# Window attention after a gated scan: exponentials head by head with a bias and a running sum, a residual folded into a product, small square roots on another engine, other planner settings

## The chip, the cores and the metric

The kernel runs on one core of one Trainium2 chip. The metric is the device time of one execution in microseconds (us). All data is 32-bit float. TensorE is PE in the profile's rows (PEld its weight loads), VectorE is DVE, ScalarE is ACT, GpSimd is POOL, and SyncE, which here only issues DMAs, is SP.

## The reference

Two layers in a row on x of 8 images x 192 channels x 64 x 64. The first projects to 384 channels, takes a 3x3 convolution by channel, makes gates from a 16-wide proxy, and runs a recurrence over 8 steps in four directions, each step reading the state of the row above, of its own and of the row below. Its outputs are summed over the directions, normed over the channels (layernorm, then GRN, a norm over the whole image), and projected back to 192. The second layer works on windows of 8x8 tokens with six heads of 32:

```python
def _layer_norm(x, g, b):
    mu = jnp.mean(x, -1, keepdims=True)
    var = jnp.mean(jnp.square(x - mu), -1, keepdims=True)
    return (x - mu) * jax.lax.rsqrt(var + EPS_LN) * g + b
...
shortcut = _layer_norm(xs, norm1_g, norm1_b)
...
attn = jnp.einsum('bhnd,bhmd->bhnm', _l2n(q), _l2n(k)) * temperature
kth = jax.lax.top_k(attn, IN_CC)[0][..., -1:]
attn = jnp.where(attn >= kth, attn, NEG)
...
attn = jax.nn.softmax(attn + rpb[None], axis=-1)
out = jnp.einsum('bhnm,bhmd->bhnd', attn, v)
...
out = out @ proj_w.T + proj_b
...
x2 = shortcut + out
hdn = _layer_norm(x2, norm2_g, norm2_b)
hdn = jax.nn.gelu(hdn @ fc1_w.T + fc1_b, approximate=False) @ fc2_w.T + fc2_b
x2 = x2 + hdn
```

`IN_CC` is 16, `NEG` is -100.

## The kernel before

**Stages.** For image 0 a prologue does the convolution with the input in SBUF: by VectorE for nine units of 16 rows x 128 channels (`convolved`, L477 and L479), by PE with diagonal weights for three (`convolved_by_products`, L489). From then on three generators write down steps for every image: `front` (projection and convolution of the next images, through a padded copy in DRAM), `scan` (the recurrence) and `window_row` (the second layer for one row of eight windows, 512 tokens; eight such rows an image, 64 in all). The windows of an image can begin only when its scan has ended, since GRN needs the whole image: while image b is scanned, the windows of image b-1 are worked on. After the last scan only windows are left.

**The planner.** `Plan` takes each step with its engine, an assumed cost, and what it reads and writes. `run` simulates the engines with these costs, and gives each engine the ready step of lowest rank; a step that is late by more than SLACK is passed over. `order` repeats this RUNS times, each time with ranks moved towards the latest start that the step's users allow, and keeps the order of the shortest plan. The instructions are then issued in that order on every engine. So the order is fixed when the kernel is built, and each engine works through its own queue in it. Buffers are given out by the same plan: PSUM has two banks for `nb` and six shared ones (`lp`, and `g` in the scan).

**A scan tile** (128 channels, one direction, one step; 96 an image): PE makes gates (`project`, L808) into PSUM; ACT takes their absolute values (L865, L887), VectorE multiplies gates by the state (L872, L874), POOL adds (L896, L913, L917), ACT takes a reciprocal through Ln and Exp (L909, L911), VectorE and POOL multiply (L924, L928, L933), VectorE writes the state (L941). For two tiles at a time PE makes the output gates, VectorE multiplies (L967, L972), and POOL adds to the sum (L979 to L989).

**A window row.** Lines that the change or the prediction touches:

- `zg` is read and scaled on ACT (L1171). PE projects tokens into PSUM `pz` (L1186). VectorE writes `s0 = pz * n1_g` (L1193), ACT squares `pz` with a running sum `ss` (L1205; reading the sum is an instruction of its own), two 128-token groups at a time.
- `rsqrt` is an inverse square root: Ln, Exp and Square on ACT (L613 to L615), then three small Newton instructions on POOL (L618 to L620). It is used for `ss` and `sd` (twice a row each, two columns), for `nn` (once a row, 48 columns) and for `gr` (once an image). Scaling by 1/192 and adding 1e-5 are POOL's (L1211, L1536).
- ACT scales `s0` by `ss` (L1219); PE transposes it into `sT` (L1151), of which there is one; `s0` has two buffers, since the residual still needs it.
- q and k are projected (L1236), normed and transposed; scores go from PSUM to `at` (L1365), 24 pairs of columns (three groups of two heads times eight windows), 64 wide.
- For each of three groups: VectorE finds the 16 largest (L1378 to L1382) and masks the rest (L1392, L1395). POOL adds the position bias (L1405), negates the maximum into `down` (L1413) and adds it (L1422). ACT takes one exponential of 512 columns (L1426). VectorE sums (L1429) and inverts (L1430); POOL multiplies (L1437).
- PE transposes and attends (L1452, L1472), and projects `oT` into `pp` (L1506). VectorE adds the residual, `x2 = pp + s0` (L1518), and takes mean and variance (L1529, L1530). ACT negates the mean (L1546), POOL multiplies it by `sd` (L1553), ACT norms (L1561).
- The MLP follows: transposes (L1574, L1576), two products with a Gelu between them (L1593, L1597, L1604, L1613), and the second with the residual added by identity products (L1627), then the output (L1641).

After each scan VectorE computes GRN's scales with eight small instructions (L1109 to L1115 and L1128 to L1135).

Of the kernel before, what the change touches and what calls it, by code (L numbers as in the profile page):

```python
# [82 lines left out]
class Plan:  # L83
# [9 lines left out]
    RUNS = 60  # L93
    SLACK = 40.0
# [56 lines left out]
    def order(self):  # L151
# [9 lines left out]
        for n in range(self.RUNS):  # L161
# [7 lines left out]
            for s in run:  # L169
                needs = [d.start for d in s.after] + [h.next.start for h in s.held if h.next]  # L170
                rank = min(needs, default=s.end) - (s.end - s.start)
                s.rank = (s.rank + rank) / 2 if n else rank
# [152 lines left out]
def tile_ss2d_then_window_attention(ctx: ExitStack, tc: tile.TileContext, a: dict, out: bass.AP):  # L325
# [62 lines left out]
    n1_g = load("n1_g", a["n1_g"].partition_broadcast(P))  # L388
# [25 lines left out]
    sT, oT = (blank(n, [P, 2, GT], 0.0) for n in ("sT", "oT"))  # L414
    for t in (sT, oT):
        nc.gpsimd.memset(t[HALF : HALF + 1, 1, :], 1.0)
# [11 lines left out]
    with early, tc.tile_pool(name="early_ps", bufs=2, space=PSUM) as early_ps:  # L428
# [53 lines left out]
        def convolved_by_products(ct, u):  # L482

            acc = epool.tile([P, 16, W], F32, name="acc_p", bufs=2)
# [11 lines left out]
        by_vector = [(ct, u) for ct, u in units if ct < CT - 1 or u == 0]  # L496
# [5 lines left out]
        for n, c in enumerate(by_vector):  # L502
            acc = convolved(*c)
            stored(*c, acc)
            if n in (4, 6, 7):
                convolved_by_products(CT - 1, (4, 6, 7).index(n) + 1)
# [53 lines left out]

        ps = prep_ps.tile([P, 512], F32, name="ps_pre")
# [7 lines left out]
        for ci in range(2):  # L569
            w = w_f1[:, ci, :]  # L570
            nc.vector.tensor_scalar(w, w, n2_g[:, ci : ci + 1], None, ALU.mult)
# [32 lines left out]
    def rsqrt(v, key, shape, name, gain=1.0):  # L604

# [5 lines left out]
        plan("ACT", tiny, lambda: nc.scalar.activation(r(), v(), AF.Ln), r=[key], w=[r])  # L613
        plan("ACT", tiny, lambda: nc.scalar.activation(r(), r(), AF.Exp, scale=-0.5, bias=log_c[gain]), w=[r])
        plan("ACT", tiny, lambda: nc.scalar.activation(sq(), r(), AF.Square), r=[r], w=[sq])  # L615

        def newton():
            nc.gpsimd.tensor_mul(v(), v(), sq())  # L618
            nc.gpsimd.tensor_scalar(v(), v(), -1.0, 3.0 * c * c, ALU.mult, ALU.add)
            nc.gpsimd.tensor_mul(v(), v(), r())  # L620

        plan("POOL", (750.0, 60.0), newton, r=[r, sq], w=[key])


    def front(b, xs, xsT):
# [48 lines left out]
        def convolve(ct, s):  # L674
# [30 lines left out]
            st = Held(fpool, [P, CH, 64], "st", bufs=2)  # L705
# [37 lines left out]
    def scan(b, xs, xsT, z, made):  # L743
# [371 lines left out]
        plan("DVE", tiny, lambda: nc.vector.tensor_mul(gn(), gn(), gr()), r=[gr], w=[gn])  # L1115
# [27 lines left out]
    def window_row(b, g, z, sc, bb):  # L1143
        def two_blocks(dst, key, src):

            for ci in range(2):
# [8 lines left out]
                plan("PE", turned(4), turn, r=[src], w=[pt])  # L1155
# [8 lines left out]

        zg = Held(lpool, [P, CT, CH, 64], "zg", bufs=1)
# [8 lines left out]
        s0 = Held(lpool, [P, NT, DM], "s0", bufs=2)  # L1174
        for t2 in range(2):
            pz = bank()
            ss = Held(small, [P, 2], "ss")
            for k in range(2):

                def tokens(t2=t2, k=k, pz=pz):  # L1180
# [10 lines left out]
                "DVE",  # L1191
                vec(2 * DM),
                lambda two=two, pz=pz: nc.vector.tensor_mul(  # L1193
                    s0()[:, two, :],
                    pz()[:, 0 : 2 * DM].rearrange("p (k m) -> p k m", k=2),
                    n1_g.unsqueeze(1).to_broadcast([P, 2, DM]),
# [5 lines left out]
            def squares(pz=pz, ss=ss):  # L1202
                for k in range(2):
                    part = pz()[:, k * DM : (k + 1) * DM]
                    nc.scalar.activation(part, part, AF.Square, accum_out=ss()[:, k : k + 1])  # L1205

            plan("ACT", (782.0, 100.0), squares, w=[pz, ss])
            plan(
                "POOL",
                tiny,  # L1210
                lambda ss=ss: nc.gpsimd.tensor_scalar(ss(), ss(), 1.0 / DM, 1e-5, ALU.mult, ALU.add),  # L1211
                w=[ss],
            )
            rsqrt(ss, ss, [P, 2], "ss")

            def scaled(t2=t2, ss=ss):
                for k in range(2):
                    part = s0()[:, 2 * t2 + k, :]
# [3 lines left out]
            yield  # L1222
        plan.lane = 7
        two_blocks(sT, "sT", s0)
# [5 lines left out]
        for tt in range(NT):  # L1230
# [9 lines left out]
            plan("PE", mm(2, DIN), projected, r=["sT"], w=[pq, (qk, "room")])  # L1240
# [27 lines left out]
        for p2 in range(2):  # L1268
# [14 lines left out]
            plan("PE", mm(4, DM), values, r=["sT"], w=[pv, (v, "room")])  # L1283
# [85 lines left out]
        for r in range(3):  # L1369
# [21 lines left out]
            def mask(rng=rng, less=less):  # L1391
# [19 lines left out]
                "POOL",  # L1411
                tiny,
                lambda rng=rng: nc.gpsimd.tensor_scalar(down()[:, rng], top()[:, rng, 0], -1.0, None, ALU.mult),  # L1413
# [5 lines left out]
            plan(  # L1419
                "POOL",  # L1420
                gp(512),
                lambda part=part, rng=rng, each=each: nc.gpsimd.tensor_add(part(), part(), each(down()[:, rng])),  # L1422
                r=[(down, r)],
                w=[(at, r)],
            )
            plan("ACT", act(512, 95.0), lambda part=part: nc.scalar.activation(part(), part(), AF.Exp), w=[(at, r)])  # L1426

            def denominators(part=part, rng=rng):
                nc.vector.tensor_reduce(rd()[:, rng], part(), AX.X, ALU.add)  # L1429
                nc.vector.reciprocal(rd()[:, rng], rd()[:, rng])  # L1430

            plan("DVE", (833.0, 83.0), denominators, r=[(at, r)], w=[(rd, r)])
# [63 lines left out]
        x2, xn = (Held(lpool, [P, NT, DM], n, bufs=1) for n in ("x2", "xn"))  # L1496
        for t2 in range(2):
            pp = bank()
            two = slice(2 * t2, 2 * t2 + 2)
            stats, mv, sd = Held(small, [P, 2, 6], "stats"), Held(small, [P, 2, 2], "mv"), Held(small, [P, 2], "sd")  # L1500

            def projected(t2=t2, pp=pp):
# [269 lines left out]
```

## Time and profile before

| | us |
|---|---|
| median of 3 runs | 7552.91 (7535.86 to 7554.57) |
| profiled execution, its own time | 7551.0 |
| its span, first to last instruction | 7549.2 |
| mean granted TensorE clock | 0.864 of full speed |

The page gives the busy time of each engine, the span in 40 slices, and groups of instructions by line. A group's row reads: line, engine, operation, output<-input (partitions x elements), count, then busy time and the mean of one, then how long the engine stood idle just before them and for whom. The slices show where the stages change:

```profile
PE   7888799898989899888999899989888888898887
PEld 3333344444444444444445444444444444444554
DVE  6787798988899889898898988889899988899543
ACT  3555377765676567675777757776666656666765
POOL 1898788998899989987988888889899989899422
PEclk8887699987988889898988889987888878888999
```

Each digit is a slice of 189 us in tenths; PEclk is the granted clock. The costliest groups that belong to the window rows' part under the change are small beside the scan's:

```profile
L896 POOL TENSOR_TENSOR ab<-ab 128x512 f32<-128x512 f32 x672 | 866.0, 1289 | 163.1 <-ACT ab L865 151.5
L1422 POOL TENSOR_TENSOR at<-at,down 128x512 f32<-128x512 f32 x192 | 201.7, 1051 | 3.5
L1429 DVE TENSOR_REDUCE rden<-at 128x8 f32<-128x512 f32 x192 | 129.4, 674 | 42.5 <-ACT at L1426 42.4
L1426 ACT ACTIVATE at<-at 128x512 f32<-128x512 f32 x192 | 121.1, 633 | 69.8 <-POOL at L1422 69.2
```

### The profile page before, as it was taken

The page shows a single profiled execution, that of the slowest core. Times are in us where ns is not written, and L with a number is a line of the kernel's source. Part 1 is how long each engine was busy: PE and PEld are TensorE (multiplying, and loading weights), DVE is VectorE, ACT ScalarE, POOL GpSimd, SP SyncE. Part 2 cuts the span into 40 slices and gives each one's busy share as a digit, 9 for nine tenths or more (in the row PEclk, how much of TensorE's full clock was granted, in tenths as well). Part 3 has the DMA queues.
Part 4 walks back from the last instruction along what each step waited for, and adds up shares of the span by engine and source line. Part 5 has one row for each costly group of instructions (what it writes and reads, how often), then busy time and mean ns, then how long its engine had stood idle before and what let it go on. Part 6 is the DMA issues. An engine that isn't in the chain of part 4 may idle for free. (4 is left out here: it accounts for less than half of the span.)

```text
span 7549.2 us, 141750 instructions
## 1 busy us (share of the span) xinstructions
PE 6680.5 (88%) x50180; PEld 3448.8 (46%) x50180; DVE 6360.6 (84%) x15477; ACT 4895.1 (65%) x9649; POOL 6227.8 (82%) x6333
## 2 busy tenths in 40 slices
PE   7888799898989899888999899989888888898887
PEld 3333344444444444444445444444444444444554
DVE  6787798988899889898898988889899988899543
ACT  3555377765676567675777757776666656666765
POOL 1898788998899989987988888889899989899422
PEclk8887699987988889898988889987888878888999
DMA  5666354313541246213641144411121121111110
GB/s 165 163 174 162 108 154 124 81 50 100 157 120 50 68 133 158 65 49 94 162 117 44 53 121 132 119 47 53 54 55 48 45 67 44 50 45 45 32 22 14
DMA packets 988330, 669.39 MB, mean 89 GB/s; under 512 B 651971, under 2 KB 814214, under 8 KB 987622
## 3 DMA queue, kind: packets, MB, share of 16 engines
q1 hardware_dynamic: 986486, 658.87, 32.5%
q8 instruction: 398, 6.52, 0.4%
q14 instruction: 310, 2.54, 0.1%
q10 hardware_dynamic: 1136, 1.47, 0.1%
HBM read 433.98 MB, written 226.18 MB: 87 GB/s over the span
## 5 line engine op out<-in xcount | busy, mean ns | idle before, releaser
L808 PE MATMUL g<-xe,w_g 32*128 32x512 f32 x3648 | 1165.2, 749 | 228.5 <-DVE dx L967 80.5
L808 PE MATMUL g<-xo,w_g 32*128 32x512 f32 x3648 | 1201.7, 730 | 186.3 <-DVE dx L967 95.6
L865 ACT ACTIVATE ab<-g 128x512 f32<-128x512 f32 x1344 | 784.9, 596 | 397.9 <-PE nb L808 169.6
L896 POOL TENSOR_TENSOR ab<-ab 128x512 f32<-128x512 f32 x672 | 866.0, 1289 | 163.1 <-ACT ab L865 151.5
L928 POOL TENSOR_TENSOR pw<-pw,rr 128x512 f32<-128x512 f32 x672 | 865.9, 1289 | 134.7 <-ACT rr L911 113.7
L913 POOL TENSOR_TENSOR pw<-pw,pq 128x512 f32<-128x512 f32 x672 | 881.6, 1312 | 77.7 <-DVE pq L872 52.0
L917 POOL TENSOR_TENSOR pw<-pw,pq 128x512 f32<-128x512 f32 x672 | 877.4, 1306 | 15.5
L909 ACT ACTIVATE rr<-nb,eps 128x512 f32<-128x512 f32 x672 | 461.9, 687 | 577.9 <-DVE nb L906 575.3
L981 POOL TENSOR_TENSOR dx<-dx,hu 128x512 f32<-128x512 f32 x576 | 743.0, 1298 | 111.0 <-DVE hu L972 94.2
L808 PEld LDWEIGHTS g<-xo,w_g 32*128 32x128 f32 x3648 | 412.8, 207 | 726.8 <-DVE dx L967 200.3
L808 PEld LDWEIGHTS g<-xe,w_g 32*128 32x128 f32 x3648 | 407.2, 212 | 702.9 <-DVE dx L967 179.4
L1627 PE MATMUL lp<-hd,w_f 128*64 128x256 f32 (+1 forms) x2304 | 604.7, 502 | 57.2 <-ACT hd L1613 15.0
L989 POOL TENSOR_TENSOR y<-y,dx 128x512 f32<-128x512 f32 x384 | 598.2, 1565 | 2.2
L695 PE MATMUL lp<-strip,w_cv 128*32 128x256 f32 x8064 | 566.8, 420 | 27.3 <-DMA strip<-pad 22.7
L924 DVE SCALAR_TENSOR_TENSOR nb<-nb,rr 128x512 f32<-128x512 f32 x672 | 464.0, 691 | 145.4 <-ACT rr L911 142.8
L933 DVE SCALAR_TENSOR_TENSOR nb<-nb,pw 128x512 f32<-128x512 f32 x672 | 463.6, 690 | 139.3 <-POOL pw L928 137.4
L906 DVE TENSOR_TENSOR nb<-nb,ab 128x512 f32<-128x512 f32 x672 | 464.1, 691 | 115.1 <-POOL ab L896 106.6
L972 DVE TENSOR_TENSOR hu<-g,hid 128x512 f32<-128x512 f32 x768 | 516.8, 678 | 0.9 <-PE g L808 0.6
L887 ACT ACTIVATE nb<-nb 128x512 f32<-128x512 f32 x672 | 399.5, 595 | 141.1 <-DVE pq L874 80.3
L808 PE MATMUL nb<-xe,w_g 32*128 32x512 f32 x672 | 479.1, 799 | 10.0 <-DVE hid L941 9.8
L808 PE MATMUL nb<-xo,w_g 32*128 32x512 f32 x672 | 464.1, 777 | 16.9 <-DVE hid L941 16.8
L941 DVE TENSOR_TENSOR hid<-lx,nb 128x512 f32<-128x512 f32 x672 | 454.2, 676 | 4.9
(223 smaller groups left out, 16413.8 us busy)
## 6 DMA issues: line engine op xcount, KB each, us to landing
strip<-pad SPq DMA_DIRECT2D x1008, 132.0 KB
xd<-xsT SPq DMA_DIRECT2D x384, 256.0 KB
x<-xs SPq DMA_DIRECT2D x64, 768.0 KB
xd<-xs SPq DMA_DIRECT2D x192, 256.0 KB
z<-y SPq DMA_DIRECT2D x64, 768.0 KB
zg<-z SPq DMA_DIRECT2D x64, 768.0 KB
pad<-xin SPq DMA_DIRECT2D x168, 264.0 KB
xsT<-sn SPq DMA_DIRECT2D x168, 256.0 KB
```

Of the source, the lines that this page charges most:

```text
L695: nc.tensor.matmul(pc()[q * RG : (q + 1) * RG, k * 256 : (k + 1) * 256].rearrange("p (h w) -> p h w", h=4), lhsT=w_cv[:, ct, q, dx, :], rh ...
L808: nc.tensor.matmul(dst, lhsT=w[rows, col : col + P], rhs=xp[rows, :], start=True, stop=True)
L865: lambda r=r: nc.scalar.activation(ab()[:, r, :], g[r](), AF.Abs),
L896: plan("POOL", gp(512), lambda: nc.gpsimd.tensor_add(ab()[:, 0, :], ab()[:, 0, :], ab()[:, 1, :]), w=[ab])
L906: plan("DVE", vec(512), lambda: nc.vector.tensor_add(nb(), nb(), ab()[:, 0, :]), r=[ab], w=[nb])
L913: plan("POOL", gp(512), lambda: nc.gpsimd.tensor_add(one(), one(), pq()[:, 0, :]), r=[(pq, 0)], w=[pw])
L917: lambda: nc.gpsimd.tensor_add(one(), one(), pq()[:, 1, :]),
L928: plan("POOL", gp(512), lambda: nc.gpsimd.tensor_mul(one(), one(), rr()), r=[rr], w=[pw])
L972: lambda: nc.vector.tensor_mul(like(hu(), d), like(pu(), d), state(d, ct)),
L981: plan("POOL", gp(512), lambda: nc.gpsimd.tensor_add(dx(), dx(), hu()), r=[hu], w=[dx])
L989: nc.gpsimd.tensor_add(y, y, dx().rearrange("p (c i) -> p i c", c=CH))
L1627: nc.tensor.matmul(dst[:, at : at + rhs.shape[-1]], lhsT=lhsT, rhs=rhs, **flags)
```

## The change

- **Exponential.** POOL's add of the negated maximum and VectorE's sum go. ACT takes 24 exponentials of 64 columns a row, eight to a step, each with its maximum as bias and its sum accumulated. The negation moves from POOL to VectorE, with a lower bound of -100 on the maximum.
- **Small square roots.** `rsqrt`'s Newton steps move from POOL to VectorE, two instructions in place of three, and give the negated result; the sign is taken back in weights (`n1_g`, `w_f1`, `gn`). Division and epsilon move into ACT's Ln and Square. `ss` and `sd` are treated once a row with four columns, not twice with two.
- **First norm.** `n1_g` is multiplied into weights beforehand; `s0` is a plain copy of `pz` on ACT.
- **Residual and second norm.** PE adds the residual: `sT` times a diagonal matrix `w_dg`, accumulated into `pp`; a 193rd column of both products gives the negated mean. ACT copies `x2` and the mean out of PSUM and takes the variance as a square with a running sum. `sT` gets a second buffer, `s0` and `st` lose theirs.
- **Prologue.** One more unit of the convolution on PE, one fewer on VectorE.
- **Planner.** 12 plans in place of 60, SLACK 80 in place of 40, ranks moved by 0.4 in place of 0.5.

```diff
-    RUNS = 60
-    SLACK = 40.0
+    RUNS = 12
+    SLACK = 80
...
-                s.rank = (s.rank + rank) / 2 if n else rank
+                s.rank = 0.6 * s.rank + 0.4 * rank if n else rank
...
-        by_vector = [(ct, u) for ct, u in units if ct < CT - 1 or u == 0]
+        by_vector = [(ct, u) for ct, u in units if ct < CT - 1]
...
         def newton():
-            nc.gpsimd.tensor_mul(v(), v(), sq())
-            nc.gpsimd.tensor_scalar(v(), v(), -1.0, 3.0 * c * c, ALU.mult, ALU.add)
-            nc.gpsimd.tensor_mul(v(), v(), r())
+            nc.vector.scalar_tensor_tensor(v(), v(), eps * mean, sq(), ALU.add, ALU.mult)
+            nc.vector.scalar_tensor_tensor(v(), v(), 3.0 * c * c, r(), ALU.subtract, ALU.mult)
-        plan("POOL", (750.0, 60.0), newton, r=[r, sq], w=[key])
+        plan("DVE", (160.0 + 4 * math.prod(shape[1:]) / 0.96, 85.0), newton, r=[r, sq], w=[key])
...
-                lambda rng=rng: nc.gpsimd.tensor_scalar(down()[:, rng], top()[:, rng, 0], -1.0, None, ALU.mult),
+                lambda rng=rng: nc.vector.tensor_scalar(down()[:, rng], top()[:, rng, 0], NEG, -1.0, ALU.max, ALU.mult),
...
-                lambda part=part, rng=rng, each=each: nc.gpsimd.tensor_add(part(), part(), each(down()[:, rng])),
-            plan("ACT", act(512, 95.0), lambda part=part: nc.scalar.activation(part(), part(), AF.Exp), w=[(at, r)])
-                nc.vector.tensor_reduce(rd()[:, rng], part(), AX.X, ALU.add)
+            for i0 in range(r * WS, (r + 1) * WS, 8):
+                def powers(i0=i0):
+                    for i in range(i0, i0 + 8):
+                        row = at()[:, i, :]
+                        nc.scalar.activation(
+                            row, row, AF.Exp, bias=down()[:, i : i + 1], accum_out=rd()[:, i : i + 1]
+                        )
+                plan("ACT", (290.0 * 8, 95.0), powers, r=[(down, r), (at, r)], w=[(at, r, i0), (rd, r, i0)])
...
+                    for j in range(2):
+                        cols = slice(at + j * HALF, at + j * HALF + more)
+                        nc.tensor.matmul(pp()[:, cols], lhsT=sT[:, j, tok], rhs=w_dg[:, j, :], start=False, stop=j == 1)
...
-                lambda two=two, pp=pp: nc.vector.tensor_add(
+                nc.scalar.copy(
+                    x2()[:, 2 * t2 : 2 * t2 + 2, :].rearrange("p k (j m) -> p k j m", j=2),
...
-                    nc.vector.bn_stats(stats()[:, k, :], x2()[:, 2 * t2 + k, :])
-                    nc.vector.bn_aggr(mv()[:, k, :], stats()[:, k, :])
+                    nc.scalar.activation(
+                        xn()[:, k, :], x2()[:, k, :], AF.Square, bias=less_m()[:, k : k + 1], accum_out=sd()[:, k : k + 1]
+                    )
```

## The prediction

> **What bounds the kernel now.** I read the page's busy line first, then the table of stages, then who VectorE waits for, then single rows.
>
> ```profile
> PE 6680.5 (88%) x50180; PEld 3448.8 (46%) x50180; DVE 6360.6 (84%) x15477; ACT 4895.1 (65%) x9649; POOL 6227.8 (82%) x6333
> ```
>
> Three engines are close together and ScalarE (ACT) has room. The stages, cut at the ends of the first and the last image's scan (found by the GRN reduction at L1109, at 938 and 7030 us):
>
> ```profile
> 60.00:938.00 878.00, 713.94 (x4537) 302.76 (x4536) 661.28 (x1017) 427.19 (x707) 657.26 (x519) 0.77 0.57 152
> 938.00:7030.00 6092.00, 5475.67 (x41528) 2849.64 (x41529) 5425.99 (x13275) 4116.09 (x8214) 5407.01 (x5457) 0.87 0.31 84
> 7030.00:7549.00 519.00, 437.72 (x3986) 277.12 (x3984) 228.41 (x1146) 327.40 (x698) 148.21 (x321) 0.93 0.10 21
> ```
>
> Columns: stretch, length, busy time of PE, PEld, DVE, ACT, POOL, granted clock, DMA. From 938 to 7030, where scan and windows overlap, PE is busy 90%, VectorE 89%, GpSimd (POOL) 89%, ACT 68%. In the last 519 us only windows run: PE 84%, ACT 63%, the two others under 45%. The change touches windows only, so the first 938 us hardly move. The same table for L1426 alone puts 164 of its 192 instructions (three to a window row) before 7030: 54.7 of the 64 rows lie in the middle stage, 9.3 in the tail. VectorE's longest waits in the middle stage:
>
> ```profile
> DVE nb L933 <- POOL pw L928: 105.4, 103, 4.8
> DVE nb L924 <- ACT rr L911: 103.2, 96, 5.4
> DVE nb L906 <- POOL ab L896: 69.7, 86, 4.4
> DVE pq L872 <- PE nb L808: 62.4, 55, 4.1
> ```
>
> Summed over all its waits there: POOL 193.2, ACT 206.5, PE 203.6 us. No engine alone is the bound; the scan's chain runs through all four.
>
> **The change, part by part, in busy time for a window row.** *POOL loses* the add of the negated maximum (L1422, 201.7 us over 64 rows), the negation (L1413, 59.0), every small Newton and scaling instruction of the three square roots (L618 to L620 on ss, sd and nn: 82.9, 76.9 and 52.1; L1211 26.0, L1536 28.1, L1553 25.4): 552.1, or 8.6 us a row, 470 in the middle stage. It falls there from 5407 to 4937, 81%.
>
> *VectorE loses* L1193 and L1518 (69.6 each), L1529 and L1530 (86.5, 46.5) and the sum over the powers, L1429 (129.4): 401.6, or 6.28 a row. *It gains* ten small instructions a row: two for each of three square roots, a product for less_m, three negations. Their price decides the case, and all ten are of a kind that this kernel hardly issues: every operand in SBUF, two of them in seven and one in the negations. The nearest are the scales after a scan:
>
> ```profile
> 950.36 1.18 DVE L1131 TENSOR_TENSOR sc<-sc,vecs 128x3 f32<-128x3 f32 x1
> 951.58 1.19 DVE L1132 TENSOR_SCALAR sc<-sc 128x3 f32<-128x3 f32 x1
> ```
> ```profile
> 950.26 1.27 POOL L896 TENSOR_TENSOR ab<-ab 128x512 f32<-128x512 f32 x1
> 951.48 1.27 POOL L981 TENSOR_TENSOR dx<-dx,hu 128x512 f32<-128x512 f32 x1
> ```
>
> Columns: start, duration. Three columns wide, each ends with the POOL instruction that runs beside it; over the eight scans L1131 takes 164 ns at least and 1181 in the median. L1128 and L1129, a PSUM source and a reciprocal, take 148 and 164 always. The wider L1392, two SBUF operands, takes 639 at least and 1014 in the mean: a wait of 375 ns. Scaled by POOL's new share (81/89) a first such instruction waits 0.35; a second one right behind finds POOL's next just begun and waits 0.8 (1.02 from L1131, scaled so). The floor is 0.15 for two operands, 0.17 for one. A square root's pair is then 1.45, three are 4.35; less_m 0.5; three negations at 0.52 are 1.56. Sum 6.4 against 6.28 removed: nothing is gained on VectorE, +7 us in the middle stage. Bounds: all at their floors 1.6 a row (-258 us), all at L1132's mean of 1163 ns 11.6 (+293). I stay between, since the wider two-operand row does.
>
> The Trainium skill ("GPSIMD Engine Reference", Specifications) lists GpSimd's SBUF interfaces as shared with VectorE, in contention with instructions in a two-port mode or with two SBUF inputs. That speaks against this move, and the rows above agree with it; read as full exclusion it would put the sum at the upper bound, without it at the lower.
>
> *ACT gains* 24 exponentials of 64 columns with a bias and a running sum, and loses three of 512 (0.53 each from start to next start). No row has this form. The pair of a square and the reading of its sum, without bias:
>
> ```profile
> 7006.42 0.32 ACT L1205 ACTIVATE lp<-lp 128x192 f32<-128x192 f32 x1
> 7006.67 0.18 ACT L1205 ACTIVATION_READ_ACCUMULATOR lp<-lp 128x1 f32 x1
> 7006.88 0.32 ACT L1205 ACTIVATE lp<-lp 128x192 f32<-128x192 f32 x1
> ```
>
> It takes 0.40 a pair (two in 0.80); at 0.88 ns a column (L1038 against L614, 403 and 292 ns for 128 and 2 columns) the 128 columns fewer take off 0.11: 0.29 at least. L1067, with bias and scale, starts every 0.81; less 448 columns 0.41 at most. One pointer lies between: 0.35. So 24 x 0.35 - 3 x 0.53 = +6.8. Four copies of 384 columns replace VectorE's work (0.38 from start to start, L1252 to L1244): +1.5. Four squares with sums for the variance, 0.40 each: +1.6. Two square roots in place of four: two trios of 0.40 fewer, -0.8. Together +9.1 a row, 499 us in the middle, 85 in the tail; ACT goes from 4116 to 4615 there (76%). By the skill ("ScalarE: Activation LUTs", What ACT_TABLE_LOAD costs) a bias pointer adds about 93 ns to an instruction; its formula gives an estimate of some 240 ns for the power alone behind another, and no price for reading the sum. This does not enter the sum.
>
> *PE gains* eight products of 97 columns a row. L1506 takes 208.8 us for 512 of 192: 0.41 each, so 0.21 for 97. With one more column on each old product, 1.67 a row: 91 us in the middle, 15 in the tail. No order hides it on a PE that is 90% busy.
>
> *Waits.* VectorE waits for others; each wait grows or shrinks with the awaited engine's load. In proportion to busy time: POOL -17, ACT +25, PE +3, together +11. In proportion to busy over idle: POOL 7.9 to 4.3, -88; ACT 2.08 to 3.12, +103; PE 8.9 to 10.6, +39; together +54. I take the middle, +32. Behind a block of eight exponentials (2.8 us instead of 0.5) stand the scan's Abs, Ln and Exp (L865, L887, L909) and the emptying of PSUM banks; who waits for them are POOL's L896, VectorE's L924 and PE.
>
> *Tail.* POOL and VectorE are idle there, so taking work off them gains only shorter hops; PE's 15 us lie on the bound, ACT's 85 fit into its 192 idle us, but PE waits 72.6 us for ACT already. Bounds 0 and 105 (its waits scaled by ACT's busy over idle, 1.7 to 3.8, and the 15 on top); I take 25, nearer the lower, since the hops shorten.
>
> *Start.* One of nine convolutions (0.81 + 8 x 1.285 = 11.1 us) moves from VectorE to PE; ACT empties PE's behind the others, so I take -6 of 0 to -11. The single st buffer is priced by its neighbour sn, single already: ACT waited 2.8 us for it in all, so nothing. Doubling sT takes a wait off PE that its rows barely show (6.3 us at L1236): nothing. No DMA is added or moved to another queue.
>
> *Order.* The planner's other settings deal the instructions out anew; what that is worth no row shows. Stages of equal content (2645 to 3525 and 3525 to 4425, 24 of L1426 each) last 880 and 900: 10 either way, 70 over seven if all fell alike. I take 0.
>
> **Sum.** Profiled execution 7551.0 (span 7549.2 and 1.8 around it; the median of the runs is 7552.9): -6 start, +7 VectorE, +32 waits, +25 tail: **7609**, +0.8%.
>
> **Rivals.** *The relief counts* (not slower): the ten instructions cost 0.4 each, 4.0 a row, since a lighter POOL leaves gaps: -125 in the middle; POOL's waits fall by the full 88 and ACT's grow only in proportion, +25 with PE's +3 and so -60. 7551 - 125 - 60 - 6 + 25 = 7385; with half of the wait relief 7415. For it: POOL was the fullest beside VectorE, and L1131 does fall to 164 when POOL is idle. Against: POOL stays at 81%. I put it at 7400. *ACT's blocks decide*: 3 x 54.7 = 164 blocks, each 2.3 us longer; if half of them hold up a scan instruction that is awaited, 189 us instead of the +32: 7551 - 6 + 7 + 189 + 25 = 7766. From 14 blocks on (32 over 2.3) it outweighs the estimate of the waits. For it: 103 us are waited for L911 already. Against: ACT idles 24% after. *Nothing shows*: the upper half of the wait estimate is wrong, the new order repays the tail, 7551.
>
> **Numbers.** Chances: the sum 0.46 (own range 7540 to 7690), the relief 0.33, ACT's blocks 0.13, nothing 0.08. Some 0.3% (23 us) is what a measurement tells from no change. Faster takes the relief and a sliver of the sum and of nothing, 0.35; same most of "nothing" and the sum's lower edge, 0.11; slower the rest, 0.54. The range 7380 to 7740 leaves out under half of the relief and half of ACT's blocks.
>
> **What would show it.** VectorE's busy time near 6320 (6361 - 11 at the start, +7 in the middle, -42 in the tail, where the ten cost their floors), with the new small instructions at 0.5 to 1.0 us in the middle stage; POOL near 5670; ACT near 5480 with exponentials 0.35 apart; PE near 6785. I am wrong if the small instructions stay near 0.2 (VectorE near 6050, then faster), or if the exponentials start 0.41 or more apart and the scan's Ln waits behind them.

## The result, and the profile after

| | us |
|---|---|
| changed kernel, median of 4 runs | 7671.36 (7655.16 to 7687.0) |
| kernel before, same chip, median of 4 runs | 7550.53 |
| ratio, with 95% interval | 1.0163 [1.0142, 1.0185] |
| profiled execution after: span, mean granted clock | 7671.8, 0.866 |

The change makes the kernel slower by 121 us; the forecast was +56 against the median. The busy line of the page after:

```profile
PE 6798.8 (89%) x51240; PEld 3551.6 (46%) x51240; DVE 6332.3 (83%) x15176; ACT 5406.4 (70%) x12915; POOL 5707.9 (74%) x4584
```

VectorE is where it was (6361 before), POOL has lost 520 us, ACT has gained 511. The stages after, cut at the first and the last GRN reduction (now L1119); columns: stretch, length, busy time and count of PE, PEld, DVE, ACT, POOL, granted clock, DMA share, GB/s:

```profile
0.00:880.30 880.30, 772.95 (x4680) 314.91 (x4680) 697.31 (x1060) 448.09 (x740) 674.84 (x559) 0.83 0.61 164
880.30:7145.10 6264.80, 5598.11 (x42938) 2964.49 (x42938) 5462.77 (x13140) 4593.16 (x11123) 4972.32 (x3962) 0.87 0.31 82
7145.10:7671.80 526.70, 427.79 (x3622) 272.19 (x3622) 172.21 (x977) 365.14 (x1053) 60.78 (x64) 0.88 0.09 20
```

The first scan became 57 us shorter (937.7 before), the middle 173 longer (6092), the tail 7 longer (519.5): 123 in all. The loss lies in the middle and hides a gain at the start. There, VectorE's waits; columns: who waits for whom, us in total, times, longest:

```profile
DVE nb L934 <- ACT rr L921: 181.4, 143, 6.0
DVE pq L882 <- PE nb L818: 89.3, 67, 11.2
DVE nb L943 <- POOL pw L938: 69.7, 86, 2.6
DVE nb L916 <- POOL ab L906: 65.2, 74, 4.5
...
DVE rden L1436 <- ACT at L1430: 37.9, 29, 3.3
```

L934, L943, L916 are what L924, L933, L906 were before. The wait for ACT's reciprocal went from 103 to 181, that for POOL's `pw` from 105 to 70. Summing every row of this view by the awaited engine gives the ledger on which most of the rest stands. Busy time and waits of VectorE nearly fill the stage, so a stage that grows must show it in one or the other:

| middle stage, us | length | VectorE busy | waits | for ACT | for POOL | for PE |
|---|---|---|---|---|---|---|
| before | 6092 | 5426 | 624 | 202 | 193 | 204 |
| after | 6265 | 5463 | 768 | 375 | 142 | 242 |

Busy +37, waits +144: ACT +173, PE +38, POOL -51, DMA -16. What POOL no longer does became idle time: its own waits in the middle stage rose from 577 to 1221 us, for VectorE from 299 to 759. The largest of them after:

```profile
POOL pw L938 <- ACT rr L921: 260.5, 182, 6.5
POOL ab L906 <- ACT ab L875: 179.3, 117, 16.3
POOL y L989 <- DVE hu L982: 173.4, 79, 14.3
POOL dx L991 <- DVE hu L982: 120.6, 85, 4.9
```

What a wait for `rr` looks like, in the timeline of ACT after; columns: start, duration, instruction:

```profile
1366.19 0.69 ACT L919 ACTIVATE rr<-nb,eps 128x512 f32<-128x512 f32 x1
1366.78 0.48 ACT L1522 COPY x<-lp 128x384 f32<-128x384 f32 x1
1367.15 0.17 ACT L1531 COPY less_m<-lp 128x2 f32<-128x2 f32 x1
1367.21 0.58 ACT L1337 COPY four<-lp 96x512 f32<-96x512 f32 x1
1367.70 0.45 ACT L1538 ACTIVATE xn<-x,less_m 128x192 f32<-128x192 f32 x1
1368.06 0.19 ACT L1538 ACTIVATION_READ_ACCUMULATOR xn<-x,less_m 128x1 f32 x1
1368.15 0.44 ACT L1538 ACTIVATE xn<-x,less_m 128x192 f32<-128x192 f32 x1
1368.49 0.19 ACT L1538 ACTIVATION_READ_ACCUMULATOR xn<-x,less_m 128x1 f32 x1
1368.59 0.61 ACT L921 ACTIVATE rr<-rr 128x512 f32<-128x512 f32 x1
```

and the instruction on VectorE that waited for it, with its idle time in brackets:

```profile
1369.23 0.70 DVE L934 SCALAR_TENSOR_TENSOR nb<-nb,rr 128x512 f32<-128x512 f32 x1 [3.08 <-ACT rr L921]
```

Between the Ln and the Exp of one reciprocal stand 1.8 us of work for the windows; 1.3 of them (L1522 and L1538) are new on ACT. The planned order put them there, and the scan's chain stands still meanwhile.

The small instructions, grouped with shapes kept apart, VectorE in the middle stage (count | busy, mean ns | idle before):

```profile
L1419 DVE TENSOR_SCALAR down<-top 128x8 f32<-128x8 f32 x168 | 83.5, 502 | 0.0
L630 DVE SCALAR_TENSOR_TENSOR nn<-nn,nn_r 128x48 f32<-128x48 f32 x56 | 51.5, 919 | 1.9
L630 DVE SCALAR_TENSOR_TENSOR sd<-sd,sd_r 128x4 f32<-128x4 f32 x55 | 47.4, 861 | 1.9
L629 DVE SCALAR_TENSOR_TENSOR sd<-sd,sd_q 128x4 f32<-128x4 f32 x55 | 45.6, 830 | 4.3 <-ACT sd_q L626 4.3
...
L1545 DVE TENSOR_TENSOR less_m<-less_m,sd 128x4 f32<-128x4 f32 x55 | 30.3, 552 | 0.3
```

and one of them in the tail, where POOL works 12% of the time:

```profile
L630 DVE SCALAR_TENSOR_TENSOR sd<-sd,sd_r 128x4 f32<-128x4 f32 x9 | 1.5, 163 | 0.3
```

0.86 us beside a busy POOL, 0.16 without. All eight groups of small instructions together (three are not shown) take 359.6 us for the 56 rows in the middle stage: 6.4 a row. Taken one by one over the whole span, 198 of the 640 instructions meet no instruction of POOL, and these last 0.11 to 0.21 us. The 341 that last over 0.3 us all end 16 to 72 ns after an instruction of POOL has ended; of all of VectorE's instructions 5% do. So what they take beyond their floor is a wait for POOL's instruction, for the one-operand L1419 too.

The exponential's two groups on ACT, whole span:

```profile
L1430 ACT ACTIVATE at<-at,down 128x64 f32<-128x64 f32 x1536 | 511.0, 338 | 116.4 <-DVE down L1419 88.3 <-POOL at L1411 26.8 <-DVE lx L867 0.8
L1430 ACT ACTIVATION_READ_ACCUMULATOR at<-at,down 128x1 f32 x1536 | 293.0, 191 | 0.0
```

The two overlap: in a block the exponentials start 0.33 us apart, and the time in which either runs is 528 us, 0.344 for each. ACT now waits 88 us for the negation on VectorE, where it waited 69 for POOL's add.

### The profile page after: what moved, and what is told of

Read it like the earlier page. It is cut to its first block, busy times and chain, and to the rows that moved or that the text cites. A ratio compares the mean times of both kernels' runs of the same rounds, so it can differ in the third digit from the quotient of the medians.

```text
span 7671.8 us, 145557 instructions
## 1 busy us (share of the span) xinstructions
PE 6798.8 (89%) x51240; PEld 3551.6 (46%) x51240; DVE 6332.3 (83%) x15176; ACT 5406.4 (70%) x12915; POOL 5707.9 (74%) x4584
## 4 chain that ended last, share of the span: by engine, by line
DVE 18%; PE 16%; ACT 9%; POOL 5%; issue 3%; DMA 1%; SPq 0%; ACTq 0%; DVEq 0%; POOLq 0%
PE g L818 4%; PE lp L1616 2%; ACT at L1430 2%; DVE rest L1386 2%; PE lp L1582 1%; DVE nb L943 1%; DVE top L1384 1%; DVE kth L1388 1%; DVE nb L916 1%; DVE dx L977 1%; DVE less L1398 1%; DVE hu L982 1%; POOL pw L938 1%; DVE hid L951 1%; PE lp L1512 1%
## 5 line engine op out<-in xcount | busy, mean ns | idle before, releaser
L818 PE MATMUL g<-xe,w_g 32*128 32x512 f32 x3648 | 1148.7, 728 | 210.5 <-DVE dx L977 58.0
L818 PE MATMUL g<-xo,w_g 32*128 32x512 f32 x3648 | 1149.8, 727 | 176.6 <-DVE dx L977 68.2
L906 POOL TENSOR_TENSOR ab<-ab 128x512 f32<-128x512 f32 x672 | 867.6, 1291 | 200.4 <-ACT ab L875 196.5
L1616 PE MATMUL lp<-hd,w_f 128*64 128x256 f32 (+1 forms) x2304 | 643.6, 529 | 74.3 <-ACT hd L1602 54.0
L818 PEld LDWEIGHTS g<-xo,w_g 32*128 32x128 f32 x3648 | 392.0, 207 | 683.9 <-DVE dx L977 154.6
L934 DVE SCALAR_TENSOR_TENSOR nb<-nb,rr 128x512 f32<-128x512 f32 x672 | 464.7, 692 | 210.6 <-ACT rr L921 207.9
L1430 ACT ACTIVATE at<-at,down 128x64 f32<-128x64 f32 x1536 | 511.0, 338 | 116.4 <-DVE down L1419 88.3
L1411 POOL TENSOR_TENSOR at<-at,rpb 128x512 f32<-128x512 f32 x192 | 244.5, 1274 | 453.7 <-DVE top L1384 238.5
L943 DVE SCALAR_TENSOR_TENSOR nb<-nb,pw 128x512 f32<-128x512 f32 x672 | 464.4, 691 | 97.8 <-POOL pw L938 94.2
L916 DVE TENSOR_TENSOR nb<-nb,ab 128x512 f32<-128x512 f32 x672 | 464.2, 691 | 86.2 <-POOL ab L906 77.3
L1616 PEld LDWEIGHTS lp<-hd,w_f 128*64 128x64 f32 (+1 forms) x2304 | 294.1, 183 | 426.5 <-issue 245.2
```

What stands on the lines that cost most here:

```text
L818: nc.tensor.matmul(dst, lhsT=w[rows, col : col + P], rhs=xp[rows, :], start=True, stop=True)
L906: plan("POOL", gp(512), lambda: nc.gpsimd.tensor_add(ab()[:, 0, :], ab()[:, 0, :], ab()[:, 1, :]), w=[ab])
L1430: nc.scalar.activation(row, row, AF.Exp, bias=down()[:, i : i + 1], accum_out=rd()[:, i : i + 1])
L1616: nc.tensor.matmul(dst[:, at : at + rhs.shape[-1]], lhsT=lhsT, rhs=rhs, **flags)
```

## The experiments

Three theories. *S*: ScalarE's longer queue (the exponentials in blocks of eight above all) holds up the scan. *V*: the small instructions cost VectorE what the sums gave it. *O*: the loss is the new order that the planner makes, whatever the work.

Two ways of undoing a part were used, because an edit also changes the plan. *In the order kept*, only what a planned step issues is changed: no step moves, but the order was made for the other version. *Planned anew*, the steps themselves change, and the order with them. The kernel before, run beside each version, had medians of 7544 to 7551; a ratio is against the one beside it. Differences between versions carry these 7 us.

### In the order kept

**One exponential in place of eight, in the changed kernel.**

```diff
-                    for i in range(i0, i0 + 8):
-                        row = at()[:, i, :]
-                        nc.scalar.activation(
-                            row, row, AF.Exp, bias=down()[:, i : i + 1], accum_out=rd()[:, i : i + 1]
-                        )
+                    part = at()[:, i0 : i0 + 8, :]
+                    nc.scalar.activation(part, part, AF.Exp)
+                    nc.scalar.copy(rd()[:, i0 : i0 + 8], top()[:, i0 : i0 + 8, 0])
```

> The changed kernel with its order of instructions kept, but each block of eight exponentials with bias and sum is one exponential of 512 columns and one tiny copy (the maximum is not subtracted and the sums are not taken, so the softmax is not the reference's). This takes some 2.1 us off 192 blocks on ScalarE and nothing else. Theory S (ScalarE's longer blocks make the scan wait): VectorE's wait for ScalarE in the middle stage falls from 379 us to near 200, time 7500 to 7570. Theory V (the small instructions, now on VectorE beside a busy GpSimd): 7640 to 7670. Theory O (the planner dealt out a worse order): 7640 to 7670, since the order is the same.

Measured 7585.49, ratio 1.0056 [1.0041, 1.0071]: 86 us less than the changed kernel, just outside S's range. ACT's busy time falls to 5035, and VectorE's waits for ACT in the middle stage from 375 to 306, not to near 200. S holds, but explains a part only: in the middle stage this kernel waits for ACT 104 us more than the one before.

**The small instructions issued on POOL, in the changed kernel** (the Newton steps, `less_m`, the negation).

```diff
-            nc.vector.scalar_tensor_tensor(v(), v(), eps * mean, sq(), ALU.add, ALU.mult)
-            nc.vector.scalar_tensor_tensor(v(), v(), 3.0 * c * c, r(), ALU.subtract, ALU.mult)
+            if eps:
+                nc.gpsimd.tensor_scalar(v(), v(), eps * mean, 1.0, ALU.add, ALU.mult)
+            nc.gpsimd.tensor_mul(v(), v(), sq())
+            nc.gpsimd.tensor_scalar(v(), v(), 1.0, -3.0 * c * c, ALU.mult, ALU.add)
+            nc.gpsimd.tensor_mul(v(), v(), r())
...
-                lambda rng=rng: nc.vector.tensor_scalar(down()[:, rng], top()[:, rng, 0], NEG, -1.0, ALU.max, ALU.mult),
+                lambda rng=rng: nc.gpsimd.tensor_scalar(down()[:, rng], top()[:, rng, 0], -1.0, None, ALU.mult),
...
-        plan("DVE", (70.0, 85.0), lambda: nc.vector.tensor_mul(less_m(), less_m(), sd()), r=[sd], w=[less_m])
+        plan("DVE", (70.0, 85.0), lambda: nc.gpsimd.tensor_mul(less_m(), less_m(), sd()), r=[sd], w=[less_m])
```

> The changed kernel with its order kept, but the Newton steps, the product for less_m and the negation of the maximum are issued on GpSimd in the same places. VectorE should lose about 390 us of busy time, GpSimd gain about 270. Theory V: 7540 to 7620. Theories S and O: 7650 to 7690, as GpSimd's own queue takes them up.

Measured 7606.17, 1.0081 [1.0066, 1.0096]: 65 us less. Its busy line:

```profile
PE 6763.0 (89%) x51240; PEld 3542.3 (47%) x51240; DVE 6024.3 (79%) x14520; ACT 5402.5 (71%) x12915; POOL 5936.4 (78%) x5568
```

VectorE loses 308 us of work, POOL takes 229 more (390 and 270 were expected). In the middle stage VectorE's busy time falls by 293 and its waits rise by 236 (POOL 142 to 309). V holds; what the relief is worth in an order that was not made for it is 65.

**Eight exponentials in place of one, in the kernel before** (zero bias, sums into a spare tile).

```diff
-            plan("ACT", act(512, 95.0), lambda part=part: nc.scalar.activation(part(), part(), AF.Exp), w=[(at, r)])
+            plan("ACT", act(512, 95.0), lambda rng=rng: [
+                nc.scalar.activation(at()[:, i, :], at()[:, i, :], AF.Exp, bias=zero[:, 0:1], accum_out=spare[:, i : i + 1])
+                for i in range(rng.start, rng.stop)
+            ], w=[(at, r)])
```

> The kernel before with its order kept, but each exponential of 512 columns is issued as eight of 64 with a bias of zero and a sum into a spare tile: some 2.2 us more on ScalarE in 192 places, nothing taken off elsewhere. Theory S: VectorE waits 100 to 170 us more for ScalarE in the middle stage, time 7650 to 7730. Theories V and O: 7550 to 7590.

Measured 7775.85, 1.0304 [1.0287, 1.0321]: +231 us over the kernel before beside it (7544), past S's range, for 381 us of busy time on an engine that was 65% busy. The middle stage grows by 179 and the tail by 56; VectorE's waits in the middle grow by 157, 144 of it for ACT. The cause is ACT, with nothing else changed on any engine. Two of VectorE's waits in the middle stage:

```profile
DVE nb L925 <- ACT rr L912: 132.9, 114, 5.8
DVE rden L1433 <- ACT at L1428: 59.3, 37, 3.3
```

Before, the first was 103 us and the second, the wait of VectorE's sums for the exponentials, hardly there:

```profile
DVE rden L1429 <- ACT at L1426: 3.0, 6, 1.2
```

**The residual's products left out, in the changed kernel.**

```diff
-                    for j in range(2):
-                        cols = slice(at + j * HALF, at + j * HALF + more)
-                        nc.tensor.matmul(pp()[:, cols], lhsT=sT[:, j, tok], rhs=w_dg[:, j, :], start=False, stop=j == 1)
```

> The changed kernel with its order kept and the 512 products of 97 columns left out (x2 lacks the residual and the mean is incomplete, so the output is not the reference's). TensorE loses some 105 us of busy time, 1.67 a window row. If TensorE's new work lies on the path, as the prediction's row-by-row reading had it for the tail and left it to the wait estimate in the middle: 7570 to 7620. If it is hidden: 7650 to 7675.

Measured 7635.74, 1.0112 [1.0097, 1.0127]: 36 us less, between the two expectations. In the middle stage PE's busy time falls by 39, not by the 91 that I had priced for these products, and the stage by 17.

### Planned anew, one part at a time

**The planner's settings alone, in the kernel before.**

```diff
-    RUNS = 60
-    SLACK = 40.0
+    RUNS = 12
+    SLACK = 80
...
-                s.rank = (s.rank + rank) / 2 if n else rank
+                s.rank = 0.6 * s.rank + 0.4 * rank if n else rank
```

> The kernel before with the changed kernel's planner settings alone (12 plans, SLACK 80, 0.4). Theory O: 7630 to 7700. Theories S and V: within 20 us of 7551. In either case the first scan's end tells whether its 57 us gain (938 to 880) belongs to the planner.

Measured 7615.89, 1.0094 [1.0079, 1.0109], between the two expectations: +71 us from the order alone against the 7544 beside it, +65 against the 7550.5 of the result. The first scan ends at 896 in place of 938, so most of the gain at the start is the settings', not the prologue's; the middle stage and the tail give it back with interest (6152 and 567).

**The old settings, in the changed kernel** (the same lines, reversed).

```diff
-    RUNS = 12
-    SLACK = 80
+    RUNS = 60
+    SLACK = 40.0
```

> The changed kernel with the planner settings of before (60 plans, SLACK 40, ranks moved by half). Those settings alone cost the kernel before 71 us (7616 against 7544). Theory O (they cost the same here): 7590 to 7615, the first scan's end back near 938. Theory of luck (each order falls its own way, some 50 us either way): anywhere from 7600 to 7740, with no link to the 71.

Measured 7782.91, 1.0313 [1.0295, 1.0332], above both ranges. The settings cost the old work 65 us and save the new work 112: what an order costs depends on the work, and O falls as a term of its own.

**The exponential alone, in the kernel before** (old settings; POOL's add and VectorE's sum go, the negation moves to VectorE).

```diff
-                lambda part=part, rng=rng, each=each: nc.gpsimd.tensor_add(part(), part(), each(down()[:, rng])),
...
-            plan("ACT", act(512, 95.0), lambda part=part: nc.scalar.activation(part(), part(), AF.Exp), w=[(at, r)])
...
+                plan("ACT", (290.0 * 8, 95.0), powers, r=[(down, r), (at, r)], w=[(at, r, i0), (rd, r, i0)])
```

> The kernel before with the changed exponential and negation alone, planned anew with its own settings. Theory S: ScalarE's blocks cost more than GpSimd's and VectorE's relief returns, 7580 to 7650. If the relief outweighs the blocks once the planner knows of them: 7480 to 7540.

Measured 7683.72, 1.0179 [1.016, 1.0197]: +133 us, S's way but past its range, though POOL and VectorE have less to do.

**The exponential as before, in the changed kernel** (the same lines, reversed).

```diff
+                lambda part=part, rng=rng, each=each: nc.gpsimd.tensor_add(part(), part(), each(down()[:, rng])),
...
-                plan("ACT", (290.0 * 8, 95.0), powers, r=[(down, r), (at, r)], w=[(at, r, i0), (rd, r, i0)])
```

> The changed kernel with the exponential and the negation as before (adds and negation on GpSimd, one exponential of 512 columns, the sums on VectorE), planned anew. ScalarE falls by some 430 us of busy time, GpSimd rises by 260, VectorE by 60. Theory S: 7560 to 7610, as with the order kept (7585 without the blocks, less what GpSimd's return costs). If the exponential as such was a gain for VectorE and GpSimd that outweighed the blocks: 7680 to 7740.

Measured 7593.58, 1.0061 [1.0042, 1.008]: 78 us less than the changed kernel, and still slower than the one before.

**The norms, the residual and the prologue alone**: the exponential as before, the small instructions on POOL, the old settings. Against the kernel with the exponential as before, beside the settings:

```diff
-        plan("DVE", (160.0 + 4 * math.prod(shape[1:]) / 0.96, 85.0), newton, r=[r, sq], w=[key])
+        plan("POOL", (1000.0 if eps else 750.0, 60.0), newton, r=[r, sq], w=[key])
...
-        plan("DVE", (70.0, 85.0), lambda: nc.vector.tensor_mul(less_m(), less_m(), sd()), r=[sd], w=[less_m])
+        plan("POOL", tiny, lambda: nc.gpsimd.tensor_mul(less_m(), less_m(), sd()), r=[sd], w=[less_m])
```

> The changed kernel with the exponential as before, the Newton steps, less_m and the negation planned and issued on GpSimd, and the planner settings of before. What is left of the change: the copies and variances on ScalarE, the residual on TensorE, square roots once a row, the prologue. If the three costs found so far (86 for the blocks, 65 for the small instructions, 71 for the settings) are all there is, the rest of the change is a gain: 7671 - 86 - 65 - 71 = 7449, so 7430 to 7500. If they overlap: 7500 to 7560.

Measured 7502.61, 0.9942 [0.9924, 0.996]: faster than both kernels, but short of the 7449 that the three costs gave if they only add; it lies at the edge of "they overlap".

**The same with the new settings** (the settings' lines as in the change).

```diff
-    RUNS = 60
-    SLACK = 40.0
+    RUNS = 12
+    SLACK = 80
```

> The version that beat the kernel before (exponential, negation and small instructions as before, norms and residual as changed: 7503 us), now with the changed kernel's planner settings. Those settings ended the first scan 40 to 57 us sooner in every run so far, and cost the kernel before 71 us over all, but spared the changed kernel 112. If the first scan's gain is all that carries over: 7450 to 7480. If the loss of the kernel before repeats: 7550 to 7590.

Measured 7400.39, 0.9798 [0.9784, 0.9813], the fastest of all and below both expectations. Its busy line:

```profile
PE 6699.2 (91%) x51240; PEld 3502.8 (47%) x51240; DVE 6127.7 (83%) x14712; ACT 5030.5 (68%) x10035; POOL 6137.5 (83%) x5760
```

VectorE has 205 us less to do than in the changed kernel, ACT 376 less, POOL 430 more.

**Eight exponentials in place of one, in that kernel's order** (the same edit as above).

```diff
+                nc.scalar.activation(at()[:, i, :], at()[:, i, :], AF.Exp, bias=zero[:, 0:1], accum_out=spare[:, i : i + 1])
```

> The best version (7400) with its order kept, but each exponential of 512 columns issued as eight of 64 with a bias of zero and a sum into a spare tile; nothing is taken off elsewhere. In the kernel before the same edit cost 231 us. Theory S: 7550 to 7650. If that price was due to the order of the kernel before alone: 7430 to 7500.

Measured 7612.93, 1.0086 [1.0071, 1.0101]: +213 us, where the other order gave +231. Two of its waits of VectorE in the middle stage:

```profile
DVE nb L938 <- ACT rr L925: 195.9, 164, 7.7
...
DVE rden L1442 <- ACT at L1437: 90.6, 44, 7.3
```

Without the blocks:

```profile
DVE nb L937 <- ACT rr L924: 169.5, 140, 7.8
...
DVE rden L1438 <- ACT at L1435: 12.9, 15, 3.0
```

The stage grows by 199, VectorE's busy time by 7, its waits by 192, 154 of them for ACT.

### Is it luck of the order?

**SLACK 70 in the changed kernel.**

```diff
-    SLACK = 80
+    SLACK = 70
```

> The changed kernel with SLACK 70 in place of 80 and nothing else, so the same work in another order. Theory of luck: the time moves by 30 us or more either way. If orders of one setting family are equally good: within 15 us of 7671.

Measured 7770.95, 1.0288 [1.0271, 1.0305]: +100 us, with the work untouched.

**The planner told nearer the true cost of an exponential.**

```diff
-                plan("ACT", (290.0 * 8, 95.0), powers, r=[(down, r), (at, r)], w=[(at, r, i0), (rd, r, i0)])
+                plan("ACT", (345.0 * 8, 95.0), powers, r=[(down, r), (at, r)], w=[(at, r, i0), (rd, r, i0)])
```

> The changed kernel with the cost that the planner assumes for one exponential raised from 290 to 345 ns, near the measured 344, and nothing else. If the loss comes from an order planned for exponentials that are too short: 7590 to 7640. If it is the work itself that ScalarE has to do: 7650 to 7700, or as far from 7671 as the run with SLACK 70.

Measured 7659.42, 1.0144 [1.0129, 1.0159]: 12 us less, inside what any new order does. The underestimate of 290 against 344 isn't the cause.

Since one order can mislead by 100 us, three more versions were run with SLACK 70, to compare each part under two settings.

```diff
-    SLACK = 80
+    SLACK = 70
```

In the kernel before with the new settings:

> The kernel before with the new planner settings but SLACK 70: a third order of its work (7550 with its own settings, 7616 with SLACK 80). If a new order moves any kernel by some 100 us: 7600 to 7720. If orders of the same settings agree: 7600 to 7630.

In the norms, residual and prologue alone:

> The best version so far (norms and residual as changed, exponential and small instructions as before; 7400 with SLACK 80, 7503 with the old settings), with SLACK 70. If the work decides and the order adds some 50 either way, it stays under the kernel before: 7380 to 7520. If the 7400 was a lucky order: above 7530.

In the changed kernel with the exponential as before:

> The changed kernel with the exponential as before and its small instructions still on VectorE, with SLACK 70 (7594 with SLACK 80). Against the version without these instructions (f2, same settings) it shows their price in a second order: theory V 60 to 200 us above f2. Against the changed kernel with SLACK 70 (7771) it shows the exponential's price: theory S 70 to 180 us below.

Measured 7669.26 (1.0162 [1.0147, 1.0178]), 7474.44 (0.9903 [0.9888, 0.9917]) and 7652.94 (1.0137 [1.012, 1.0154]). All of it as a ladder, each step's difference in brackets:

| median, us | SLACK 80 | SLACK 70 | old settings |
|---|---|---|---|
| before | 7616 | 7669 | 7550 |
| + norms, residual, prologue | 7400 (-216) | 7474 (-195) | 7503 (-48) |
| + small instructions to VectorE | 7594 (+193) | 7653 (+179) | |
| + exponential and negation: the change | 7671 (+78) | 7771 (+118) | 7783 |

Under both new settings every step has the same sign and a similar size. Under the old settings the norms' gain is only 48 us. The way from 7550 to 7671 is then: the new order on the old work +65, norms and residual -216, small instructions +193, exponentials +78. The first term holds for this path alone: with the change's work the same settings save 112.

The ledger of the middle stage along the first column shows where each step acts:

| us | length | window rows in it | VectorE busy | waits | for ACT | for POOL | for PE | VectorE busy, whole span |
|---|---|---|---|---|---|---|---|---|
| before, new settings | 6152 | 53.0 | 5394 | 719 | 244 | 223 | 236 | 6367 |
| + norms, residual, prologue | 5992 | 54.0 | 5222 | 740 | 274 | 220 | 232 | 6128 |
| + small instructions | 6153 | 53.3 | 5442 | 683 | 276 | 159 | 232 | 6379 |
| + exponential: the change | 6265 | 56.0 | 5463 | 768 | 375 | 142 | 242 | 6332 |

The norms' gain is VectorE's work (-172), the small instructions' loss is VectorE's work (+220, against 57 of waits spared), and the exponentials' loss is waiting for ACT (+99). The order also moves rows of windows between the middle and the tail, so a stage's length and busy time are partly a matter of rows (counted by the inverses of the sums, three a row); the last step's middle holds 2.7 rows more, and over the whole span its VectorE has 47 us less to do, not 21 more. Of the 173 us by which the wait for ACT grew, 42 came with the settings, 30 with the norms and 99 with the exponentials.

## Why the prediction was half right

**Right.** The direction, and the range. The engines' totals: VectorE near 6320 (6332), POOL 5670 (5708), ACT 5480 (5406), PE 6785 (6799). The price of the ten small instructions, 6.4 a row from rows that were only near them: measured 6.4, with means of 0.5 to 0.92 us each in the middle stage. The Trainium skill ("GPSIMD Engine Reference", Specifications) says that instructions of VectorE with two SBUF inputs contend with GpSimd; 0.86 against 0.16 for the same instruction agrees. The exponential: 0.35 predicted, 0.344 measured. The rival *relief counts* fell for the reason given against it: POOL went to 79% of the middle stage, and the small instructions met it all the same.

**Wrong: the waits, the term of +32.** "I take the middle, +32" between +11 and +54 is the step that failed: VectorE's waits grew by 144. POOL's part (-51) and PE's (+38) lay within their bounds; ACT's was +173 against +25 to +103. I scaled each wait by the awaited engine's load, as if the queue behind ACT only grew denser. The two tests in place (eight exponentials for one) refute that form: 323 and 330 us more on ACT in the middle stage raised the waits for it by 144 and 154, to 1.7 and 1.6 times what they were, while busy over idle rose only from 2.1 to 2.4 in the first and from 2.4 to 2.8 in the second.

What the runs show in its place: two fifths to a half of the new wait is that of the windows' own sums for the exponentials (L1433 and L1442), in the kernel before 3 us of the 202 for ACT, which no scaling by load makes large. It rose by 56 us of the 144 and by 78 of the 154. The scan's reciprocal took 30 and 26 of the rest, its absolute values 40 and 35. From the ladder's third line to the changed kernel, of 99 us the inverse of the sums took 32 (6 to 38), the scan's reciprocal 35 (146 to 181). There a block in front of the scan can be seen: in the changed kernel 20 of the 143 waits for the reciprocal, 34 us, have exponentials between the step of VectorE that feeds the Ln (L916) and the Exp; with the exponential as before 1 of 131 has. So 2.8 us in one piece do hold the chain, but in few places.

The rival *ACT's blocks decide* named these blocks and put the waits at 189, nearer to 144 than my sum; but it had half of 164 blocks hold up the scan, and only 99 of the 173 us came with the exponentials, so its nearness is in part luck. Its time, 7766, lies 92 above the profiled run (7674): the start took 51 us less than it had, the middle 23 and the tail 18.

**Wrong: start and order.** I gave the start -6 and the order 0, with a bound of 70. The start gained 57; under the settings alone, in the old kernel, it gained 41. With the old settings the kernels with the new prologue end the first scan at 933 (norms alone) and 930 (the whole change), 4 to 8 us before 938: the -6 for the prologue fits, and what the term lacked is what the settings do there. The order on the old work cost 65 in all, within the bound, but the bound's basis was poor: two like stretches of one order differ by 20, while whole orders of the same work differ by up to 119 (before: 7550, 7616, 7669; changed: 7671, 7771, 7783). The kernel before has the best of its three orders, which its profile cannot show.

**Wrong in detail.** VectorE's busy time in the middle stage rose by 37, not 7, but 56 rows in place of 54.7 fell in it. At the 21.5 us of VectorE that a row takes in the tail after (172 us for 8), 1.3 rows are some 29 us by estimate: row for row the +7 about held. The tail cost 7 and not 25, with those 1.3 rows fewer; by the row it went from 55.7 us (519.5 for 9.3) to 65.8 (526.7 for 8), +10 where I had under 3. So that term was too small as well, and rows that moved to the middle hid it; the exponentials alone take the same 9.3 rows from 519.5 to 575.5 in the kernel before. PE's 91 us of new work in the middle, left inside the +3 to +39 of its waits, were worth 36 us in the whole span.

**Errors that met.** By its parts the sum was worse than its total: -57 at the start and +144 in waits lie 51 and 112 from their terms, with opposite signs. And the change looked like one trade of work between engines; under the new settings it is a gain of about 200 us (norms and residual) with two losses on top, which no sum over engines' totals had separated. There the three come to +55 against the kernel before; that this is what I forecast is chance.

**Open.** The fastest kernel has a granted clock of 0.885 against 0.871 for the same kernel with eight exponentials, and PE is busy 6699 against 6797 us on the same products. Whether the clock is a part of its gain or follows from its shape no run here tells; between these two, VectorE's waits for PE make 27 of the 192 us by which its waits grew. The norms' gain was only measured with a new order, never in place. How many microseconds of the replanned differences are order and how many are work is known only to the spread between the columns of the ladder. And no run took the exponential with bias and sum in fewer, longer instructions.

## What to carry to other kernels

Price a move between engines in the ledger of the engine that paces the stage, busy time and waits by releaser. Some 380 us more on a ScalarE that idled a third of the time cost over 200 here: VectorE's queue, which carries scan and windows alike, waited for the new blocks themselves and for the scan's steps that stood behind them on ScalarE. Tiny instructions moved to VectorE beside a busy GpSimd are no relief: here four columns cost 0.86 us in place of 0.16, since most of these instructions wait for one of GpSimd to end. Where a planner deals out the order, test parts under two settings at least, and undo them both in place and planned anew; then take the parts apart, since the best version (7400 us) was the change without its exponentials and without the small instructions' move.

## What the hardware showed

- Exponentials of 64 columns with bias and sum start 0.33 us apart, though their records last 0.31 to 0.38 and the reading of the sum 0.19 more: reading and next exponential overlap. By the Trainium skill ("ScalarE: Activation LUTs", What ACT_TABLE_LOAD costs) a 64-column power with a bias pointer lasts an estimated 333 ns and overlaps the next instruction by 93. The duration agrees with the row (334 ns in the median), and so does the overlap: the reading starts 0.24 after its exponential. The next exponential starts 0.09 after the reading.
- The second of two small instructions in a row waits longer than the first: L630 takes 698 and 919 ns in the mean on `ss` and `nn`, L629 520 and 590. Only on `sd` are they alike (861 and 830).
- A one-operand instruction on 8 columns (L1419) takes 502 ns in the middle stage, nearly as much as one with two operands (L1545, 552). The 55 of its 192 records that meet no instruction of POOL take 0.12 to 0.17 us, so it too waits for POOL.
